# A graph layer on one core: the order of the first blocks, and a block's list of destinations spread by one full-width product

## The chip, the core and the metric

The kernel runs on one core of one Trainium2 chip. The core has five engines with queues of their own: PE (TensorE, matrix products), DVE (VectorE), ACT (ScalarE), POOL (GpSimd) and SP (SyncE, which here only issues transfers). Each engine works through its instructions in the order in which the program lists them, and waits on semaphores for the others. ACT, POOL and SP also issue DMA transfers. The metric is the device time of one execution in microseconds (us), as the median of several runs; one more execution was taken with the hardware profiler.

## What is computed

One layer of a graph network with a layer norm in front. There are 12,500 nodes with 64 features and 212,500 edges, sorted by their second end `dst` (the inputs are sorted so). Cut to what matters:

```python
h = relu(layernorm(x))                              # (12500, 64)
edge_in = concatenate([h[src], h[dst], weight])     # (212500, 129)
e = silu(edge_in @ eW1 + eb1)                       # (212500, 128)
e = silu(e @ eW2 + eb2)
agg = segment_sum(e, src, 12500)                    # sum over the edges of each first end
z = silu(concatenate([h, agg]) @ nW1 + nb1)
out = x + z @ nW2 + nb2
```

## The kernel before, in words

The first product is split by linearity. For each node the kernel projects `h` once with the upper half of `eW1` (table `ta`, for `src`) and once with the lower half (table `tb`, for `dst`), each as a rounded part and a remainder, so that a row has 2 x 128 numbers. Nodes are dealt to 100 buckets (`NB`), 125 to each.

**First half: edges to buckets.** The edges, in the order of `dst`, are cut into 208 blocks of 1024 (`BLK`); two blocks make a pair. Because `dst` is sorted, the 2048 edges of a pair need only a short stretch of rows of `tb`. `load` (L347) reads four windows of 60 rows of that stretch (`STEP` = 25 apart) into the tile `win`, two windows on partitions 0 to 59 and two on 64 to 123; next to them on each half stand three rows for the edge weight (two parts) and the bias. For each block `count` (L364) makes the list on DVE: which bucket each edge has (`oh`, `each`), how many came before it (`terms`, `rank`), and so the row of the buffer `q` to which it goes (`to`). `spread` (L337) puts the destinations of the block, as offsets into the windows (`rowsD`), on all partitions with two products, one for each half of 64 partitions, each with a column of the identity as its weights; `picked` (L373) compares them with the partition's own number (`same`) and adds the edge weights (`extras`). That gives `pick`, with one column for each edge. `send` (L440) multiplies `pick` with `win` on PE (`qp`), copies the result and the edge's place in its bucket to `qs` on ACT, and scatters the 128 rows of each tile to `q` with an indirect DMA on POOL (L476). `send_all` (L497) interleaves `send(s)` with `count(s + 1)` in three pieces for each block, and calls `load(s + 2)`.

**Second half: buckets to sums.** The buckets are read back from `q` in 14 levels (`LEVELS`), four buckets at a time, as soon as a level can no longer get rows (`fetch`, L523). A pipeline of steps (`turn`, L654) adds the `ta` row of the first end (`s_pt`), applies the two `silu` and the second product (`s_p2`, with the bias tile `b2f`), and sums by node with a one-hot product (`s_seg`). The last level continues into the node product (`nodes`, L274).

**The order.** PE, DVE, ACT and SP are scheduled by hand: instructions stand in the order in which the Python code makes them. The main loop (L886) walks over the steps and, at each `None` of `turn`, draws pieces of `send_all` so that each level's blocks are done when it starts. The projection of the nodes (`loaded`, `normed`, `products`, called the feed here) comes as generators through `turns`, and a fixed number of turns is drawn for each piece.

**The start.** The first blocks must not wait for all of `tb`. So 16 rows of x for each partition (`x0`, 2048 nodes) are loaded first, normalised (`norm`, L658) and projected by four calls of `first_rows` (L689) into a table of their own, `tb0`, which the windows of the first 30 blocks (`EARLY`) are read from. `sources` (L765) turns `src` into bucket and place (`bkt`, `locE`) for one half of each pair at a time; `destinations` (L742) makes the bases of the pairs' windows (`base_i`, read by SP at L355) and the offsets `rowsD`; `edge_weights` (L784) splits the weights into two parts, the second by a subtraction on POOL, and writes both to `ews`, from which `load_rows` (L328) reads each pair's `extras`. All of them have one pair on each partition (104 pairs, `NP`). `order` (L829) lists in which sequence turns of these generators stand, before the first block. `checks` (L792) makes sure that every destination lies in its window; if not, a slow general path runs at the end.

Of the kernel before, what the change touches and what calls it, by code (L numbers as in the profile page):

```python
# [28 lines left out]
F32 = mybir.dt.float32  # L29
# [48 lines left out]
def tile_gnn(ctx: ExitStack, tc: tile.TileContext, x, src, dst, ew, eW1, eb1, eW2, eb2, nW1, nb1, nW2, nb2, out):  # L78
# [48 lines left out]
    NE, EARLY = 16, 30  # L127
# [9 lines left out]
    dstR = lp.tile([NP, PAIR], I32, name="dstR")  # L137
    f, sf, t = (lp.tile([NP, PAIR], F32, name=n) for n in ("f", "sf", "t"))
    fv = f.rearrange("p (g e) -> p g e", e=HALF)
    lo = lp.tile([NP, 4], F32, name="lo")  # L140
    ewR, ewH = (lp.tile([NP, PAIR], F32, name=n) for n in ("ewR", "ewH"))
    nc.vector.memset(srcR[96:NP, LAST:], N)
    nc.vector.memset(ewR[96:NP, LAST:], 0.0)
    ones = const.tile([1, P], F32, name="ones")
# [3 lines left out]
    nc.sync.dma_start(x0, x[: NE * P, :].rearrange("(p j) d -> p j d", j=NE))  # L148
# [5 lines left out]
    for to, v, queue in ((srcR, src, nc.sync), (ewR, ew, nc.scalar), (dstR, dst, nc.sync)):  # L154
        for p0, p1 in ((0, 96), (96, NP - 1)):
            queue.dma_start(to[p0:p1, :], vec(v, p0 * PAIR, p1 - p0, PAIR))
        queue.dma_start(to[NP - 1 : NP, :LAST], vec(v, (NP - 1) * PAIR, 1, LAST))
    last = bass.AP(tensor=dst.tensor, offset=dst.offset + E - FEW, ap=[[PAD, 1], [0, PAD // FEW], [1, FEW]])
    nc.scalar.dma_start(dstR[NP - 1 : NP, LAST:].rearrange("p (r e) -> p r e", e=FEW), last)
# [25 lines left out]
    nc.vector.scalar_tensor_tensor(same, plus, -float(HB), part, op0=OP.mult, op1=OP.add)  # L185
    nc.vector.tensor_scalar(plus, same, float(WL + 2), None, op0=OP.is_equal)
# [20 lines left out]
    rowsD = const.tile([NP, 2, 2, HALF], BF16, name="rowsD")  # L207

    tb0 = dram.tile([P * NE, 2 * H], F32, name="tb0")
    ta_buckets, tb_buckets = (t.rearrange("(l b) f -> l b f", b=NB) for t in (ta, tb))  # L210
# [21 lines left out]
    base_i = const.tile([1, NP], I32, name="base_i")  # L232
    NW = 3
    wins = [const.tile([P, 2, 2, 2, H], F32, name=f"win{i}") for i in range(NW)]
    for win in wins:
        nc.vector.memset(win, 0.0)
# [15 lines left out]

    def later_weights():

        nc.gpsimd.dma_start(w2, eW2)
# [48 lines left out]
    with ExitStack() as work:  # L304
# [23 lines left out]
        def load_rows(s):  # L328

            if s < nblocks:  # L330
                p, g = s // 2, s % 2
                if g == 0:
# [4 lines left out]
        def spread(s):  # L337

            if s < nblocks:
                p, g = s // 2, s % 2  # L340
                bc = mm.tile([P, HALF], F32, name="bc", tag="mm")
                for a in range(2):
                    of = identb[:NP, p : p + 1].to_broadcast([NP, HB])
                    nc.tensor.matmul(bc[a * HB : (a + 1) * HB], of, rowsD[:, a, g], start=True, stop=True)  # L344
# [713 lines left out]
```

## Time and profile before

| | us |
|---|---|
| median of the runs (3) | 2402.55 |
| lowest, highest | 2399.72, 2406.02 |
| the profiled execution | 2402.95 |
| its span, first to last instruction | 2401.2 |

Busy time of the engines in the profiled execution: PE 2084.7 us (87% of the span), weight loads of PE 1909.0 (80%), DVE 1807.1 (75%), POOL 1655.6 (69%), ACT 1316.8 (55%). A busy PE is not a PE at its peak, because products are pipelined and the clock that it is granted changes (0.915 in the mean).

How to read the rows that follow. A row of the timeline has the start in us from the first instruction, the duration, engine, source line, operation, and what it writes and reads; in brackets stands how long its engine had been idle and what ended that. `SPq`, `ACTq` and `PEq` are the sequencers of these engines. A group has the count, busy time in total, the mean of one in ns, and the idle time ahead of it. A window has for each engine the busy time and the count, then the granted clock of PE, the busy share of the DMA engines, and GB/s. A row of waits has the total, the number and the longest.

### The profile page before, as it was taken

The page shows a single profiled execution, that of the slowest core. Times are in us where ns is not written, and L with a number is a line of the kernel's source. Part 1 is how long each engine was busy: PE and PEld are TensorE (multiplying, and loading weights), DVE is VectorE, ACT ScalarE, POOL GpSimd, SP SyncE. Part 2 cuts the span into 40 slices and gives each one's busy share as a digit, 9 for nine tenths or more (in the row PEclk, how much of TensorE's full clock was granted, in tenths as well). Part 3 has the DMA queues.
Part 4 walks back from the last instruction along what each step waited for, and adds up shares of the span by engine and source line. Part 5 has one row for each costly group of instructions (what it writes and reads, how often), then busy time and mean ns, then how long its engine had stood idle before and what let it go on. Part 6 is the DMA issues. An engine that isn't in the chain of part 4 may idle for free.

```text
span 2401.2 us, 47870 instructions
## 1 busy us (share of the span) xinstructions
PE 2084.7 (87%) x17025; PEld 1909.0 (80%) x17025; DVE 1807.1 (75%) x2852; ACT 1316.8 (55%) x2861; POOL 1655.6 (69%) x1723
## 2 busy tenths in 40 slices
PE   3777887666688889988999999999999999999997
PEld 2555676655588788888888999998999999999885
DVE  7989977766678787776877667899988888875221
ACT  3333444333355566656666767666666666666543
POOL 5667777777777777777777766777777777776110
PEclk9555698877889999999999999999999999999999
DMA  5565877666677666777777777988888888888663
GB/s 161 210 235 212 274 227 236 209 209 220 210 250 253 209 225 221 225 236 255 258 259 247 264 251 254 294 262 255 269 269 275 266 267 279 263 270 269 207 187 92
DMA packets 238859, 572.33 MB, mean 238 GB/s; under 512 B 46346, under 2 KB 98534, under 8 KB 238097
## 3 DMA queue, kind: packets, MB, share of 16 engines
q1 hardware_dynamic: 154598, 390.24, 51.8%
q0 software_dynamic: 54080, 124.64, 14.2%
q10 hardware_dynamic: 29936, 54.31, 6.9%
q8 instruction: 138, 2.26, 0.4%
q14 instruction: 107, 0.88, 0.1%
HBM read 356.62 MB, written 212.35 MB: 237 GB/s over the span
## 4 chain that ended last, share of the span: by engine, by line
PE 43%; DMA 19%; POOL 10%; DVE 7%; issue 5%; ACT 4%; SPq 1%; ACTq 0%; POOLq 0%; DVEq 0%
DMA q<-qs,to 16%; PE seg L636 10%; POOL q L476 10%; PE p L622 10%; PE pt L583 9%; PE pt L576 5%; PE qp L454 4%; PE lr L562 3%; DMA out_dram<-os 2%; PE bc L344 1%; ACT qs L466 1%; DVE one L605 1%; SPq L124 1%; ACT e L592 1%; DVE rank L414 1%
## 5 line engine op out<-in xcount | busy, mean ns | idle before, releaser
L476 POOL DMA_INDIRECT q<-qs,to x1661 | 1615.7, 973 | 565.5 <-issue 398.4
L583 PE MATMUL pt<-oneT,a 125*128 125x128 f32 (+1 forms) x2800 | 433.9, 293 | 143.1 <-ACT oneT L567 142.1
L592 ACT ACTIVATE e<-pt 128x512 f32<-128x512 f32 x450 | 268.8, 597 | 477.4 <-PE pt L583 471.9
L622 PE MATMUL p<-w,e 128*128 128x128 f32 x3600 | 513.4, 287 | 0.0
L636 PE MATMUL seg<-one,e 128*128 128x125 f32 x3600 | 508.9, 285 | 0.2 <-DVE aggT L647 0.2
L583 PEld LDWEIGHTS pt<-oneT,a 125*128 125x128 f32 x2800 | 365.8, 198 | 159.5 <-ACT oneT L567 157.8
L622 PEld LDWEIGHTS p<-w,e 128*128 128x128 f32 x3600 | 457.6, 198 | 22.4 <-issue 22.4
L636 PEld LDWEIGHTS seg<-one,e 128*128 128x128 f32 x3600 | 445.3, 195 | 28.7 <-issue 27.3
L466 ACT COPY qs<-qp 128x512 f32<-128x512 f32 x418 | 244.5, 586 | 392.3 <-DMA q<-qs,to 276.1
L647 DVE TENSOR_TENSOR aggT<-aggT,seg 128x500 f32<-128x500 f32 x325 | 218.5, 672 | 210.1 <-PE seg L636 208.0
L454 PE MATMUL qp<-win,pick 128*128 128x256 f32 x1664 | 329.1, 325 | 28.3 <-DVE pick L376 10.8
L605 DVE TENSOR_TENSOR one<-misc,qt 128x500 f32<-128x500 f32 x450 | 302.7, 673 | 60.0 <-PE seg L636 33.1
L395 DVE TENSOR_REDUCE each<-oh 128x100 bf16<-128x800 bf16 x208 | 321.1, 1544 | 7.2
L454 PEld LDWEIGHTS qp<-win,pick 128*128 128x128 f32 x1664 | 254.1, 213 | 48.2 <-issue 15.1
L576 PE MATMUL pt<-ident,qt 128*128 128x128 f32 x1800 | 276.5, 277 | 8.3 <-ACT qs L466 7.9
L626 ACT ACTIVATE e<-p 128x512 f32<-128x512 f32 x450 | 268.7, 597 | 25.6 <-PE p L622 25.2
L567 ACT CAST oneT<-lr 125x512 fp32r<-125x512 f32 x450 | 264.7, 588 | 12.8 <-PE lr L562 12.4
L616 ACT COPY p<-b2f 128x512 f32<-128x512 f32 x450 | 267.2, 594 | 0.0
L576 PEld LDWEIGHTS pt<-ident,qt 128*128 128x128 f32 x1800 | 209.6, 143 | 23.7 <-issue 12.2
L414 DVE TENSOR_REDUCE rank<-terms 128x8 f32<-128x864 f32 x208 | 219.0, 1053 | 7.2
L376 DVE SCALAR_TENSOR_TENSOR pick<-bc,same,extra 128x512 fp32r<-128x512 f32 x208 | 154.6, 743 | 82.4 <-PE bc L344 54.3
L412 DVE TENSOR_TENSOR terms<-oh,misc 128x800 f32<-128x800 bf16 x208 | 203.6, 979 | 6.2 <-PE misc L400 5.9
(142 smaller groups left out, 1662.8 us busy)
## 6 DMA issues: line engine op xcount, KB each, us to landing
a<-ta SPq DMA_DIRECT2D x350, 512.0 KB
qt<-q SPq DMA_DIRECT2D x250, 288.0 KB
qt<-q SPq DMA_DIRECT2D x100, 576.0 KB
q<-zeros ACTq DMA_DIRECT2D x25, 1080.0 KB
q<-qs,to POOLq DMA_INDIRECT x1661
win<-tb SPq DMA_DIRECT2D x208, 120.0 KB
tb<-got SPq DMA_DIRECT2D x29, 512.0 KB
q<-zeros ACTq DMA_DIRECT2D x20, 720.0 KB
```

Of the source, the lines that this page charges most:

```text
L395: nc.vector.tensor_reduce(each, oh.rearrange("p t b -> p b t"), AX.X, OP.add)
L454: nc.tensor.matmul(qp[:, t % 2, :k], halves(pick[:, t * P : (t + 1) * P]), halves(win[:, :k, v]), start=v == 0, stop=v == 1,)
L466: nc.scalar.copy(qs[:, ts, :k, :H], qp[:, ts, :k, :])
L476: ins = nc.gpsimd.indirect_dma_start(out=q[:], out_offset=bass.IndirectOffsetOnAxis(ap=to[:k, j : j + 1], axis=0), in_=qs[:k, t % 2, a, :] ...
L576: nc.tensor.matmul(pt[:, t, :], qt[:, j, :H], ident, is_transpose=True, start=t == 0, stop=False, skip_group_check=True)
L583: nc.tensor.matmul(pt[:, cols, :], halves(a[:L, b, i * H : (i + 1) * H]), halves(oneT[:, cols, :]), start=False, stop=i == 1, skip_group_c ...
L592: nc.scalar.activation(e1, pt, AF.Silu)
L605: nc.vector.tensor_tensor(one.rearrange("p (b j) l -> p b j l", j=n), spots[:, None, None, :].to_broadcast(wide), loc[:, tiles[0][1] : til ...
L616: nc.scalar.copy(p2, b2f)
L622: nc.tensor.matmul(p2[:, t, :], e1[:, t, :], w2, start=False, stop=t == G - 1, skip_group_check=True)
L626: nc.scalar.activation(e2, p2, AF.Silu)
L636: nc.tensor.matmul(item[2][:, b, :], e2[:, t, :], one[:, t, :], start=j < G, stop=j >= G * (n - 1))
```

## The change

Five things change together.

1. **The table of destinations.** `dstR`, `f` and `rowsD` no longer hold one pair on each of 104 partitions, but use all 128: partitions 0 to 63 hold, for 64 pairs, the parts of the lists that belong to the lower half of `win`, partitions 64 to 127 those for the upper half; pairs 64 to 103 are a second such table (`NT` = 2). The bases come from a small tile of each pair's first destination, `firstR`, loaded apart with rows of four bytes. `destinations` converts and subtracts one table at a time.
2. **The spread.** For each pair `load` now lets ACT write a table `sel` (128 x 128, one column of the identity for each half), and `spread` is one product over all rows and columns instead of two.
3. **The first rows.** `x0` is loaded in two parts, 512 nodes and 1536. The first call of `first_rows` writes its rows twice, to `tb0` and to `tb00`, from which the windows of the first two pairs are read. The other three calls move from the start into the feed.
4. **The order of the start.** `order` is shorter; `load(0)` and the beginning of `count(0)` come before the rest of `sources` and `later_weights`; the loads of the feed's first rows come after `count(0)`. The weights of pair 0 are read from the on-chip tiles instead of `ews`. In the first block two turns of the feed are drawn for each piece instead of four.
5. **`b2f` and `checks`.** The bias tile is loaded on POOL's queue with the other weights and multiplied before the first block is sent, instead of after the eighth. `checks` makes its reductions in eight turns, one for each quarter, instead of two.

```diff
-    for to, v, queue in ((srcR, src, nc.sync), (ewR, ew, nc.scalar), (dstR, dst, nc.sync)):
+    for to, v, queue in ((srcR, src, nc.sync), (ewR, ew, nc.scalar)):
...
+    for T in range(NT):
+        for a in range(2):
+            whole = min(HB, NP - T * HB) - (a == 1 and T == NT - 1)
+            for n0, n1 in ((0, HB // 2), (HB // 2, HB)):
+                n1 = min(n1, whole)
+                of = shown(T * HB + n0, n1 - n0, a * HALF, [[BLK, 2], [1, HALF]])
+                nc.sync.dma_start(dstR[a * HB + n0 : a * HB + n1, T], of)
+            n = min(HB, NP - T * HB)
+            nc.scalar.dma_start(firstR[a * HB : a * HB + n, T : T + 1], shown(T * HB, n, 0, [[1, 1]]))
...
+    row = const.tile([P, 2], F32, name="row")
+    nc.vector.tensor_copy(row[:, 0:1], same)
+    nc.vector.tensor_scalar(row[:, 1:2], plus, float(STEP), None, op0=OP.mult)
...
+                if s == 0:
+                    for i, v in enumerate((ewH, ewR)):
+                        for a in range(2):
+                            at = a * HB + WL + i
+                            of = v[0:1].rearrange("p (g a e) -> p g a e", g=2, a=2)[:, :, a]
+                            nc.sync.dma_start(extras[0][at : at + 1], of)
...
-                for a in range(2):
-                    of = identb[:NP, p : p + 1].to_broadcast([NP, HB])
-                    nc.tensor.matmul(bc[a * HB : (a + 1) * HB], of, rowsD[:, a, g], start=True, stop=True)
+                nc.tensor.matmul(bc, sels[p % NW], rowsD[:, p // HB, g], start=True, stop=True)
...
+                if s < 2 * FIRST_PAIRS:
+                    table, end = tb00, G * P
...
+                    of = identb[:, p % HB :: HB][:, :, None].to_broadcast([P, 2, HB])
+                    nc.scalar.copy(sels[p % NW].rearrange("p (a m) -> p a m", a=2), of)
...
+            for to in ([tb00.rearrange("(p j) f -> p j f", j=G)] if g == 0 else []) + [rows]:
+                nc.sync.dma_start(to, got.rearrange("p g k h -> p g (k h)"))
...
+            yield
+            base = lp.tile([P, NT], F32, name="base")
+            nc.vector.tensor_copy(base, firstR)
+            nc.vector.tensor_tensor(base, base, lim, op=OP.min)
+            lot = mm.tile([1, NT, P], F32, name="lot", tag="mm")
+            for T in range(NT):
+                nc.tensor.transpose(lot[:, T, :], base[:, T : T + 1], ident)
...
+            for T in range(NT):
+                if T:
+                    nc.scalar.copy(f[:, T], dstR[:, T])
...
+                for j in range(2 * NT):
+                    nc.vector.tensor_reduce(ends[:, i, j : j + 1], fv[:, j : j + 1, :], AX.X, op)
+                    yield
...
-            order = [rows_, weights, rows_, made[0], src0, made[0], src0, made[1], made[0], made[0], src0, made[1], lists_]
-            order += [made[2], made[1], made[1], src0, made[2], lists_, made[3], made[2], made[2], src0, made[3], lists_]
-            order += [made[3], made[3], src0, lists_, src1]
+            order = [rows_, rows_, made[0], src0, made[0], src0, weights, lists_, made[0], made[0], src0, src0, lists_]
+            order += [lists_, src0, src0]
             for part_ in order:
                 next(part_)
+            load(0)
+            load_rows(0)
+            for part_ in (count0, lists_, src1, count0):
+                next(part_)
             for win in wins[1:]:
                 last_rows_of(win)
             later_weights()
...
+            for _ in range(2):
+                p2 = p2p.tile([P, G, H], F32, name="p2")
+                nc.tensor.matmul(p2, ones, b2f[0:1], start=True, stop=True)
+                nc.scalar.copy(b2f, p2)
+            for _ in count0:
+                pass
+            for _ in range(2):
+                list(todo.pop(0))
             load(1)
             rest = turns(todo, 3)
-            feed = itertools.chain(itertools.islice(rest, 48), checks(), rest)
-            for _ in send_all(0, 2 * FIRST):
-                for _ in range(4):
+            feed = itertools.chain(turns(made[1:], 2), itertools.islice(rest, 40), checks(), rest)
+            for i, _ in enumerate(send_all(0, 2 * FIRST)):
+                for _ in range(2 if i < PIECES else 4):
                     next(feed, None)
```

96 lines of the change are left out of this document (50 added, 46 removed).

## The prediction

> **What bounds the kernel now.** I read the page first, then the windows of one line, then the windows of all engines, then the timeline of the start. The largest group of the page is the scatter of edge rows on POOL:
>
> ```profile
> span 2401.2 us, 47870 instructions
> L476 POOL DMA_INDIRECT q<-qs,to x1661 | 1615.7, 973 | 565.5 <-issue 398.4
> ```
>
> 1661 scatters at 0.973 us, and before most of them 0.3 us of issue. The windows of that line alone say where this pace is kept (stretch, its length, busy us, count, clock, DMA share, GB/s):
>
> ```profile
> 43.50:163.20 119.70, 73.20 (x73) 0.56 0.54 191
> 163.20:1285.00 1121.80, 853.84 (x879) 0.87 0.72 234
> 1285.00:1417.00 132.00, 100.56 (x104) 0.99 0.77 254
> 1417.00:1600.00 183.00, 124.05 (x129) 1.00 0.83 272
> 1600.00:2211.00 611.00, 464.08 (x479) 1.00 0.83 268
> 2211.00:2401.00 190.00, 0.00 (x0) 0.97 0.55 166
> ```
>
> 879 scatters in 1121.8 us and 479 in 611.0 us are both 1.276 us each: there the queue never starves. It loses time in three places only: before the first scatter; from 43.5 to 163.2, where 73 scatters need 93.1 us and 26.6 us are lost; and from 1417 to 1600, where 129 need 164.6 and 18.4 are lost. After the last one a tail of 190 us remains. So the end is start + 1661 x 1.276 + losses + tail, and the change, whose moved work lies in the first 160 us, can be read in these terms. Who sets the pace in each stretch (PE, PEld, DVE, ACT, POOL busy):
>
> ```profile
> 43.50:163.20 119.70, 80.49 (x370) 57.71 (x370) 100.98 (x173) 43.62 (x119) 73.20 (x73) 0.56 0.54 191
> 250.00:1285.00 1035.00, 846.34 (x6729) 774.78 (x6727) 787.76 (x1200) 541.06 (x1173) 787.46 (x812) 0.90 0.72 234
> 1285.00:1600.00 315.00, 307.94 (x2785) 296.14 (x2786) 238.20 (x369) 212.17 (x446) 224.60 (x232) 0.99 0.80 264
> 1600.00:2211.00 611.00, 597.83 (x5411) 571.86 (x5411) 520.80 (x801) 385.52 (x830) 464.08 (x479) 1.00 0.83 268
> ```
>
> In the first row DVE is busy 101.0 of 119.7 us and PE 80.5: DVE, which makes each block's list and also the feed (normalising and projecting the nodes), starves POOL. From 250 to 1285 PE has 18% idle while POOL is full: PE follows the scatters. From 1285 PE is 98% busy and its own bound; its program interleaves pieces and steps in a fixed order, so if POOL and PE both come to that point earlier, everything behind shifts with them.
>
> **The start.** The timeline (start, duration, engine and line; in brackets what it waited for):
>
> ```profile
> 2.56 0.91 DVE L236 MEMSET win<- 128x1024 f32 x1 [0.18 <-issue]
> 9.68 1.21 DVE L663 TENSOR_REDUCE mean<-x 128x16 f32<-128x1024 f32 x1
> 16.74 1.90 ACT L786 CAST ewH<-ewR 104x2048 fp32r<-104x2048 f32 x1 [1.59 <-DMA ewR<-in_edge_weight_dram]
> 18.79 1.23 DVE L774 SCALAR_TENSOR_TENSOR sf<-t,sf 104x1024 f32<-104x1024 f32 x1
> 21.83 4.54 POOL L787 TENSOR_TENSOR ewR<-ewR,ewH 104x2048 f32<-104x2048 f32 x1
> 30.94 0.33 SPq L696 DMA_DIRECT2D tb<-got  x1
> 31.96 0.98 DVE L387 TENSOR_TENSOR oh<-misc,bkt 128x800 bf16<-128x800 f32 x1
> 37.08 1.01 SPq L360 DMA_DIRECT2D win<-tb  x2
> 38.20 1.14 SPq L335 DMA_DIRECT2D extra<-ews  x4
> 40.42 0.75 DVE L376 SCALAR_TENSOR_TENSOR pick<-bc,same,extra 128x512 fp32r<-128x512 f32 x1 [3.30 <-DMA extra<-ews]
> 43.52 1.90 POOL L476 DMA_INDIRECT q<-qs,to  x1 [14.59 <-ACT qs L469]
> ```
>
> DVE runs from the first mean at 9.68 to the end of the list at 37.1, then `pick` waits 3.30 us for the edge weights, and 3.1 us after it stands the first scatter.
>
> Added ahead of the mean: two memsets of 1024 elements on 32 partitions (each as the 0.91 us row, with its 0.16 gap 2.1 us) and six small ones for `row` and `lim`, some 0.15 each: +3.0 us, mean at 12.7, `sf` done at 23.0 instead of 20.0. Removed between `sf` and `oh`: three of the four `first_rows` with the waits between them. Before, that stretch is 20.0 to 32.0. Now `oh` waits for ACT, whose order is square, `sf`, root, `hr`, `got`, `ewH`, half of `f`, two `bkt`. By the rate of the `ewH` row (1.90 us for 2048 columns), `ewH` runs 22.9 to 24.8, `f` 1.0, the two `bkt` 0.5 each: `oh` at 27.0, 4.9 us earlier. The second half of `rowsD` (1.2 us) now stands after `each`: the list ends at 33.6, 3.5 earlier. Moved ahead of the first `qp` on PE are the two products for `b2f`; at 2.04 us each (row further down) with two ACT copies they end near 34.7, so they hide behind the list to within a microsecond.
>
> The new wait is data for `pick`. The weights of pair 0 come from the on-chip rows, but `ewR` needs the 4.54 us subtraction on POOL, now 24.8 to 29.4, because `ewH` is later. On SP the extras stand behind two writes of `got` (`tb00`, `tb0`), the register load and both `win` loads. Before, the last `got` write went out at 30.94 and the `win` load that waits for it at 37.08, 6.1 us for 0.5 MB, with the two 0.85 MB `ews` writes of L789 alongside. Now `got` goes out near 24, so `tb00` lands between 27 and 30; but the `ews` writes start at 29.4 and meet the `win` loads and extras (2.2 us before, from 38.20 to 40.42). Lower bound: no contention, the list decides, `pick` at 33.6. Upper: the loads wait until the `ews` writes are through, 6 to 7 us after issue, `pick` at 38. I take 36.4, nearer the upper, since the only row of the kind shows a slow landing. First scatter 39.5 instead of 43.5: **-4.0 us, bounds -6.8 to -2.4**.
> By the Trainium skill's "DMA: Bandwidth & Descriptors", section on queues, rings and completion order, each DMA engine goes round its queues packet by packet, so SP's loads would not wait for POOL's writes to be through; by that, -6.8 and a total 2.8 us lower. The 6.1 us row leans the other way.
> The queues it is moved past: SP issues ten destination loads instead of three, at about the 0.33 us of the `got` write, done before 12; ACT's queue gets four loads of 4-byte rows, for which no row exists, but they have until 24 (if late by 3 us, the list is late by 3). The `xs` loads go out after the extras, near 31 instead of 14, and are first used in block 2 or 3, near 55. POOL issues the `b2f` load and three more `win` row loads ahead of the subtraction, about 2 us, and is free near 24, as `ewH` ends.
>
> **The first blocks.** The stalls of POOL between 43.5 and 163.2, and what lies behind them:
>
> ```profile
> 54.73 1.21 POOL L476 DMA_INDIRECT q<-qs,to  x1 [5.46 <-ACT qs L469]
> 64.26 0.97 POOL L476 DMA_INDIRECT q<-qs,to  x1 [3.87 <-ACT qs L469]
> 97.77 2.29 DVE L796 TENSOR_REDUCE ends<-f 104x4 f32<-104x2048 f32 x1
> 113.57 0.97 POOL L476 DMA_INDIRECT q<-qs,to  x1 [6.36 <-ACT qs L469]
> 145.47 2.04 PE L858 MATMUL p<-b2f,ones 1*128 1x512 f32 x2 [4.83 <-DMA b2f<-in_L_gnn_eb_dram]
> 152.45 0.97 POOL L476 DMA_INDIRECT q<-qs,to  x1 [7.77 <-ACT qs L469]
> ```
>
> The costs of DVE in that window (group, busy us, mean ns, idle before):
>
> ```profile
> L395 DVE TENSOR_REDUCE each<-oh 128x100 bf16<-128x800 bf16 x10 | 15.2, 1519 | 0.3
> L414 DVE TENSOR_REDUCE rank<-terms 128x8 f32<-128x864 f32 x9 | 9.5, 1053 | 0.3
> L227 DVE TENSOR_TENSOR got<-ab,got 128x256 f32<-128x256 f32 x25 | 9.6, 417 | 3.6 <-ACT got L224 3.5
> L376 DVE SCALAR_TENSOR_TENSOR pick<-bc,same,extra 128x512 fp32r<-128x512 f32 x9 | 6.7, 742 | 7.1 <-PE bc L344 7.1
> ```
>
> The 7.77 us stall at 152.45 is the `b2f` chain: PE waited 4.83 for its DMA, multiplied twice and let `pick` wait 7.1. Loaded and multiplied before the first scatter, it is gone. The 6.36 us stall at 113.57 lies behind `checks`, which took DVE for two reductions of 2.29 us in one piece. The new one makes eight of about 0.6 us in eleven turns, four to a piece: same work, shorter holds. The two stalls of the first blocks (5.46, 3.87) came from ACT waiting on the normalisation of `xs`; now ACT has `bkt`, `locE`, `hr`, `got` there, and the second half of block 0 still needs the whole `src1` chain, so 4.4 us remain of the first and little of the second.
>
> What keeps the rest from vanishing is DVE. One list costs 5.95 us (the eight operations from `oh` to `pick`; the longest rows stand above), nine make 53.6, so 47.4 of the 101.0 are feed: checks 5.2, `src1` 3.3, and 38.9 for 93 turns, 0.42 each. After: turns in the first eight blocks are 90 (two a piece in the first block), of which 11 are checks and 12 the three moved `first_rows` (3 x 2 x 0.417 = 2.5), so 67 x 0.42 = 28.0; feed 39.0, DVE 92.6 against POOL's 91.8 for 72 scatters. With some 9 us of waits left (11.6 now without `pick`'s 7.1), DVE needs 101.6: **9.5 us lost instead of 26.6, -17.1**. Bounds: 2 lost if the waits overlap (-24.6), 19 lost if only `b2f`'s stall goes (-7.6). The feed turns not done here run over blocks 9 to 23 instead of 9 to 20, nine turns to a block: 3.8 + 5.95 us, under 10.2. If that cover failed, 0.4 us a turn would be lost.
>
> **The spread.** In the PE-bound stretch, on PE alone:
>
> ```profile
> 1450.90 0.41 PE L344 MATMUL bc<-rowsD,identb 104*64 104x512 bf16 x2
> 1451.24 1.16 PE L622 MATMUL p<-w,e 128*128 128x128 f32 x8
> 1452.23 0.40 PE L562 MATMUL lr<-identb,one 128*125 128x128 bf16 x4
> 1452.46 1.11 PE L636 MATMUL seg<-one,e 128*128 128x125 f32 x8
> ```
>
> The two half-width products take 0.34 us until the next instruction starts; four `lr` products, also 512 rows of bf16 in sum, take 0.23. One full-width product should be like the latter: 0.11 us per block, 29 blocks between 1285 and 1600 (104 + 129 scatters over 8), up to 3.2 us off the 18.4 lost there; nothing after 1600, where POOL is full. The Trainium skill's "TensorE: Matmul & The Clock Gate", part on packing small matmuls, has column tiles run side by side for the price of one; the pair starts as one entry here and agrees, and by that rule the merged product saves nothing. I take half, -1.6.
> The table costs ACT one copy of 128x128 per pair. Nearest rows:
>
> ```profile
> L469 ACT CAST qs<-locE 128x64 f32<-128x64 bf16 x414 | 105.2, 254 | 0.0
> L466 ACT COPY qs<-qp 128x512 f32<-128x512 f32 x414 | 243.5, 588 | 392.3 <-DMA q<-qs,to 276.1 <-PE qp L454 82.3 <-PE lr L562 10.6
> ```
>
> and what PE waits for on ACT between 1285 and 1600 (total, times, longest):
>
> ```profile
> PE pt L583 <- ACT oneT L567: 3.0, 1, 3.0
> ```
>
> 0.25 to 0.59 us, I take 0.3, 104 times. It is queued two blocks before its use, ahead of a `qs` eviction. Until 1285 POOL's backlog of eight `qs` tiles covers it; from 1285 ACT is two thirds busy and PE waited for it once. Cost 0; uncovered, 45 pairs x 0.3 = 13.5 us.
>
> **Sum.** -4.0 - 17.1 - 1.6 = -22.7 us. The profiled execution took 2402.95 us (span 2401.2), 0.4 above the median of 2402.55 (2399.72 to 2406.02): 2402.95 - 22.7 = 2380.3, on the median's scale **2380 us**.
>
> **Rivals.**
> *DVE gives only the named wait back* (0.17). Its work stays the pace, and the other stalls return in other places: -7.6 - 2.4 = -10, 2393 us. For it: 84% busy. Against: the moved turns take 8.4 us off DVE there.
> *The gain stops at PE* (0.06). Were PE the bound through the whole middle, an earlier scatter would only wait longer: 2402 us. Against: 18% idle from 250 to 1285.
> *ACT's copies lengthen the PE-bound half, slower* (0.06). If a copy costs like the 128x512 row and each ACT microsecond there holds back a `qs` eviction and with it PE: 45 x 0.59 = 26.5 us against 21.1 gained, 2408 us. It decides from 0.47 us exposed per pair up. Against: ACT's idle third.
> *More* (0.09). Start -6.8, first blocks -24.6, spread -3.2: -35, 2368 us.
>
> **How the numbers follow.** The forecast gets 0.62, with 2371 to 2389 as its own range. Of the -10 case most lies below the bound of faster. The range 2366 to 2396 takes in the bounds of start and first blocks and the -10 case, and leaves out the two last-named losses and part of the 2368. A change under 0.3% (7 us) can't be told from none. Faster by more than that: 0.62 + 0.09 + most of 0.17 = 0.86; within 0.3%: 0.09; slower: 0.05.
>
> **What would show it.** First scatter between 37 and 41, `pick` just before it waiting for the extras; from there to the 73rd scatter about 101 us with no stall over 5 except one after the fourth scatter; no `b2f` product after the first scatter; `checks` rows near 0.6 us; then 1.276 us each to about 1395, 15 to 18 us lost within 200 us, last scatter near 2187, the tail 190. The `bc` row should be one product of about 0.23 to 0.34 us, the table copy about 0.3. I am wrong if the first scatter is not earlier, if new stalls over 5 us appear in the first ten blocks or near 230, where the feed now meets the first steps, or if more than 22 us are lost from 1285 to 1600.

## The result, and the profile after

The median fell from 2403.45 us (four runs, 2399.72 to 2406.02) to 2385.22 us (four runs, 2383.31 to 2388.04). The ratio of the runs is 0.9928, with a 95% interval of 0.9913 to 0.9943 (the two medians alone give 0.9924). The medians differ by 18.2 us, where 22.7 were forecast. The profiled execution of after took 2388.04 us, the longest of its four, so the two traces differ by 14.9 us only, and the terms below add up to that number.

The page of after, its span and the scatters:

```profile
span 2386.3 us, 47571 instructions
L513 POOL DMA_INDIRECT q<-qs,to x1661 | 1617.5, 974 | 545.7 <-issue 396.7
```

The windows of the scatter line (stretch, length, busy us, count, clock, DMA share, GB/s), cut at the places that answer to those of before:

```profile
41.70:146.70 105.00, 73.29 (x73) 0.68 0.55 194
146.70:1268.00 1121.30, 853.88 (x878) 0.87 0.72 237
1390.00:1585.00 195.00, 133.96 (x139) 1.00 0.82 271
1585.00:2195.00 610.00, 463.62 (x478) 1.00 0.83 269
```

The first of these windows over all engines (PE, PEld, DVE, ACT, POOL):

```profile
41.70:146.70 105.00, 69.28 (x330) 52.19 (x331) 94.45 (x164) 39.54 (x110) 73.29 (x73) 0.68 0.55 194
```

Read them in the terms of the forecast. The first scatter stands at 41.70 (43.52 before): -1.8. From there the 73rd comes 105.0 us later (119.7): -14.7. From the 73rd to 1390 the lead shrinks from 16.5 to 15.3 us, +1.2: 878 scatters take 1121.3 us, 1.277 each, where 1.276 was the pace before. From 1390 to 1585, 139 scatters need 177.4 us at 1.276 and take 195: 17.6 lost instead of 18.4, and the last scatter goes out at 2193.1 (2209.2), 16.1 ahead: -0.8. The tail is 193.2 us instead of 192.0: +1.2. The sum is -14.9.

**The start.** The timeline of after:

```profile
25.34 4.52 POOL L835 TENSOR_TENSOR ewR<-ewR,ewH 104x2048 f32<-104x2048 f32 x1 [2.86 <-ACT ewH L834]
26.23 4.71 DVE L808 TENSOR_TENSOR rowsD<-f,lo 128x1024 bf16<-128x1024 f32 x1 [1.18 <-ACT f L793]
29.81 0.56 POOL L837 DMA_DIRECT2D ews<-ewH  x1
31.05 3.67 SPq L366 DMA_DIRECT2D extra<-ewR  x2
33.29 1.21 DVE L808 TENSOR_TENSOR rowsD<-f,lo 128x1024 bf16<-128x1024 f32 x1
36.98 0.17 DVE L453 TENSOR_SCALAR to<-rank 128x8 int32<-128x8 f32 x1
38.60 0.75 DVE L413 SCALAR_TENSOR_TENSOR pick<-bc,same,extra 128x512 fp32r<-128x512 f32 x1 [1.45 <-DMA extra<-ewR]
41.70 1.90 POOL L513 DMA_INDIRECT q<-qs,to  x1 [10.79 <-ACT qs L506]
```

and the same subtraction on DVE in the timeline of before:

```profile
27.80 1.22 DVE L757 TENSOR_TENSOR rowsD<-f,lo 104x1024 bf16<-104x1024 f32 x1
```

Two things are late. The first subtraction of the offsets took 4.71 us instead of 1.22 (the second, at 33.29, took 1.21 again). It runs from 26.23 to 30.94, and POOL's subtraction of the weights from 25.34 to 29.86: DVE's ends 1.08 us after POOL's, about its own duration. In before POOL's stood at 21.83 to 26.37, and DVE's first at 27.80; the new order put them side by side. So the list ends at 37.15, as in before (37.12), and not at 33.6. And `pick` then still waits, to 38.60, for the extras, so that it is these that set the first scatter: SP needed 3.67 us to issue two small loads at 31.05, while the two `ews` writes, the first of which POOL had issued at 29.81, were on their way.

**The first blocks.** The four stalls of POOL of over 1.5 us that are left, in its timeline (the scatter behind each):

```profile
50.56 0.97 POOL L513 DMA_INDIRECT q<-qs,to  x1 [3.09 <-ACT hr L723]
67.71 0.97 POOL L513 DMA_INDIRECT q<-qs,to  x1 [1.80 <-ACT qs L506]
91.85 0.97 POOL L513 DMA_INDIRECT q<-qs,to  x1 [2.98 <-ACT qs L506]
125.69 0.97 POOL L513 DMA_INDIRECT q<-qs,to  x1 [2.74 <-ACT got L248]
```

None is over 3.1 us. Those of 6.36 and 7.77 us behind `checks` and `b2f` are gone. DVE is busy 94.5 us of the 105.0.

**The spread.** PE around a block's product, before and after, at the same place of the program (timelines; x4 and x8 are runs of equal instructions):

```profile
1450.33 0.64 PE L454 MATMUL qp<-win,pick 128*128 128x256 f32 x4
```

```profile
1449.27 0.63 PE L491 MATMUL qp<-win,pick 128*128 128x256 f32 x4
1449.74 0.39 PE L377 MATMUL bc<-rowsD,sel 128*128 128x512 bf16 x1
1449.97 1.05 PE L659 MATMUL p<-w,e 128*128 128x128 f32 x8
```

Before, 0.57 us go from the first `qp` to the pair and 0.34 from the pair to what follows (1450.90, 1451.24), 0.91 in all; after, 0.47 and 0.23, 0.70. The one product saves 0.21 us, of which 0.10 lie ahead of it. Over the 58 places of this kind that each trace has in the last stretch (behind 1600 and behind 1585), the medians of the whole are 0.98 and 0.79.

### The profile page after: what moved, and what is told of

Its sections match the earlier page's. It is cut to its first block, busy times and chain, and to the rows that moved or that the text cites. A ratio compares the mean times of both kernels' runs of the same rounds, so it can differ in the third digit from the quotient of the medians.

```text
span 2386.3 us, 47571 instructions
## 1 busy us (share of the span) xinstructions
PE 2039.2 (85%) x16818; PEld 1913.8 (80%) x16818; DVE 1811.5 (76%) x2865; ACT 1336.1 (56%) x2966; POOL 1657.6 (69%) x1724
## 4 chain that ended last, share of the span: by engine, by line
PE 40%; DMA 19%; DVE 13%; POOL 9%; issue 6%; ACT 5%; SPq 2%; ACTq 0%; DVEq 0%; POOLq 0%
DMA q<-qs,to 15%; PE p L659 10%; POOL q L513 9%; PE seg L673 9%; PE pt L620 8%; PE qp L491 4%; PE pt L613 4%; DMA out_dram<-os 3%; PE lr L599 2%; DVE rank L451 2%; DVE each L432 2%; DVE one L642 1%; DVE oh L424 1%; DVE terms L449 1%; ACT qs L503 1%
## 5 line engine op out<-in xcount | busy, mean ns | idle before, releaser
L659 PEld LDWEIGHTS p<-w,e 128*128 128x128 f32 x3600 | 465.2, 200 | 15.7 <-issue 14.9
L673 PEld LDWEIGHTS seg<-one,e 128*128 128x128 f32 x3600 | 449.9, 195 | 19.2 <-issue 17.6
L424 DVE TENSOR_TENSOR oh<-misc,bkt 128x800 bf16<-128x800 f32 (+1 forms) x209 | 203.7, 975 | 2.4 <-ACT bkt L829 2.4
```

What stands on the lines that cost most here:

```text
L659: nc.tensor.matmul(p2[:, t, :], e1[:, t, :], w2, start=False, stop=t == G - 1, skip_group_check=True)
L673: nc.tensor.matmul(item[2][:, b, :], e2[:, t, :], one[:, t, :], start=j < G, stop=j >= G * (n - 1))
```

## The experiments

Nine kernels were run, in twelve runs, and all of them met chips on which the kernel before takes 1.39 to 1.42 times as long (3340 to 3422 us). From about 55 us on, engines stand there for up to 16.3 us at a time for something that the profile does not name. A row of the waits of one of them, 300 to 1270 us (total, times, longest):

```profile
ACT e L627 <- remote: 138.2, 16, 14.8
```

In after nothing of the kind stands in that stretch. The start is not touched by it: where the edit leaves after's order of the start, the first scatter is at 41.4 to 42.1 (41.70). So these runs are read for the first 60 us, for the duration of single instructions, and for ratios; single times scatter by 15 us either way and settle little.

**One input for the offsets.** To see whether the second input of DVE's subtraction is what makes it wait for POOL:

```diff
-                nc.vector.tensor_tensor(
-                    rowsD[:, T], f[:, T], lo[:, T, :, None].to_broadcast([P, 2, HALF]), op=OP.subtract
-                )
+                for g in range(2):
+                    nc.vector.tensor_scalar(rowsD[:, T, g], f[:, T, g], lo[:, T, g : g + 1], None, op0=OP.subtract)
```

> The offsets rowsD are made by four DVE subtractions with the base as a scalar for each partition (one input from SBUF) instead of two with two inputs from SBUF; nothing else changes. Theory (port): in the changed kernel the first rowsD took 4.71 us instead of 1.22 because POOL's subtraction of the edge weights ran from 25.34 to 29.86 and both read SBUF through something they share; with one input the first two run at once, about 0.6 us each, while POOL subtracts, and the list ends near 33.5 instead of 37.1. The first scatter then still moves by less than 1 us from 41.7, because pick waits for the extras of ewR (38.6) and qp for the b2f products (38.4). Rival (data): rowsD waited for something else, and takes as long here. Rival (list): the list alone set the start, and the first scatter comes 3 to 4 us earlier, at 38.

The timeline, and the durations of the four halves (min, median, max in ns):

```profile
25.63 4.52 POOL L834 TENSOR_TENSOR ewR<-ewR,ewH 104x2048 f32<-104x2048 f32 x1 [2.86 <-ACT ewH L833]
26.52 4.36 DVE L809 TENSOR_SCALAR rowsD<-f,lo 128x512 bf16<-128x512 f32 x2 [1.18 <-ACT f L793]
36.56 0.17 DVE L453 TENSOR_SCALAR to<-rank 128x8 int32<-128x8 f32 x1
38.62 0.75 DVE L413 SCALAR_TENSOR_TENSOR pick<-bc,same,extra 128x512 fp32r<-128x512 f32 x1 [1.88 <-DMA extra<-ewR]
```

```profile
L809 DVE TENSOR_SCALAR rowsD<-f,lo x4: 476/502/3910, 26.5 to 33.6; 128x512 bf16<-128x512 f32 x4
```

A miss: with one tensor input the first half still took 3.91 us, to 0.28 us after POOL's end, and only the other three took 0.5. So it is not the second input alone that makes it wait. It settles something else, though: the list ended 0.42 us earlier (36.73 instead of 37.15), and `pick` did not, 38.62. In this start the extras decide.

**The whole start without its waits.** ACT makes the offsets, the `ews` writes go out on SP behind the extras, and `b2f` is filled by a transfer alone (two products remain behind block 8, whose result is not read; the check of the windows reads the offsets):

```diff
-                if T:
-                    nc.scalar.copy(f[:, T], dstR[:, T])
-                nc.vector.tensor_tensor(
-                    rowsD[:, T], f[:, T], lo[:, T, :, None].to_broadcast([P, 2, HALF]), op=OP.subtract
-                )
+                for g in range(2):
+                    nc.scalar.activation(rowsD[:, T, g], dstR[:, T, g], AF.Identity, bias=lo[:, T, g : g + 1])
...
-                nc.gpsimd.dma_start(ews[i], v.rearrange("p (g a e) -> p g a e", g=2, a=2))
...
             load_rows(0)
+            for i, v in enumerate((ewH, ewR)):
+                nc.sync.dma_start(ews[i], v.rearrange("p (g a e) -> p g a e", g=2, a=2))
```

> The changed kernel with three waits of its start taken away at once: ACT makes rowsD straight from dstR with the negative base as its bias (no copy to f, nothing on DVE, checks reduce rowsD instead), the writes of ews go out on SP behind the extras of pair 0 instead of on POOL ahead of them, and b2f is loaded onto all partitions by DMA instead of being spread by two products (two short products only open its PSUM tiles). Theory: the list ends near 32.5 and pick waits for the extras until 33 to 35, so the first scatter stands at 36 to 38 instead of 41.7, and as DVE is the pace up to block 9 and has 2.4 us less to do, block 9 starts 4 to 7 us earlier than 146.6; this lasts to the end. Rival (landing): extras and win loads land no earlier without the ews writes beside them, pick stays at 38 and the first scatter at 41.

```profile
25.10 4.53 POOL L829 TENSOR_TENSOR ewR<-ewR,ewH 104x2048 f32<-104x2048 f32 x1 [2.36 <-ACT ewH L828]
25.85 1.33 ACT L804 ACTIVATE rowsD<-dstR,lo 128x512 bf16<-128x512 int32 x2
25.87 0.99 DVE L422 TENSOR_TENSOR oh<-misc,bkt 128x800 bf16<-128x800 f32 x1 [1.06 <-ACT bkt L823]
28.36 1.42 DVE L442 TENSOR_TENSOR alike<-bkt 128x64 bf16<-128x64 bf16 x1
30.28 1.17 SPq L364 DMA_DIRECT2D extra<-ewR  x2
32.05 0.17 DVE L451 TENSOR_SCALAR to<-rank 128x8 int32<-128x8 f32 x1
32.59 0.75 DVE L411 SCALAR_TENSOR_TENSOR pick<-bc,same,extra 128x512 fp32r<-128x512 f32 x1 [0.36 <-DMA extra<-ewR]
35.70 1.89 POOL L511 DMA_INDIRECT q<-qs,to  x1 [6.07 <-ACT qs L504]
```

The list ends at 32.22 and the first scatter stands at 35.70, 6.0 us ahead of after. Beside POOL's subtraction ACT's halves take 0.7 each. But `alike`, which compares two on-chip tables and took 0.28 in after, takes 1.42 and ends at 29.78, 0.15 us after POOL: another instruction with two inputs from on-chip tables, the same wait. `oh`, which has one input from there and one from the memory that PE writes its products to, took 0.99 beside the same subtraction (0.98 in after), so not every DVE instruction waits. No run took the subtraction off POOL; that DVE waits for it is read from the ends of these rows, 0.15 to 1.09 us behind POOL's, and from the same work at its usual length where POOL does not subtract.

**One wait of the start alone.** After, with only the two `ews` writes moved to SP behind the extras:

> The kernel of after with one thing moved: the two writes of the weights to memory go out on SP behind the extras and not on POOL ahead of them. Theory 'the writes delay the extras': the extras land within 2 us of their issue, pick follows the list at 37.2 without a wait, first scatter 40.2 to 40.4 (41.70 in after); the offsets on DVE still take 4.7 us beside the subtraction on POOL, so it does not come down to the 35.7 of the version without either. Rival 'the extras are late for another reason' (the loads of the feed, the windows, the subtraction): pick still waits for them, first scatter 41 to 42.

```profile
26.34 4.72 DVE L808 TENSOR_TENSOR rowsD<-f,lo 128x1024 bf16<-128x1024 f32 x1 [1.18 <-ACT f L793]
31.17 1.17 SPq L366 DMA_DIRECT2D extra<-ewR  x2
33.27 7.43 SPq L741 DMA_DIRECT2D xs<-in_x_dram  x4
37.09 0.17 DVE L453 TENSOR_SCALAR to<-rank 128x8 int32<-128x8 f32 x1
36.45 2.07 PE L894 MATMUL p<-b2f,ones 1*128 1x512 f32 x2 [0.68 <-ACT b2f L895]
37.28 0.75 DVE L413 SCALAR_TENSOR_TENSOR pick<-bc,same,extra 128x512 fp32r<-128x512 f32 x1
38.45 1.22 PE L491 MATMUL qp<-win,pick 128*128 128x256 f32 x4
40.74 1.54 POOL L513 DMA_INDIRECT q<-qs,to  x1 [10.77 <-ACT qs L506]
```

Issuing the two loads takes 1.17 us instead of 3.67, and `pick` follows the list without a wait. The first scatter stands at 40.74 instead of 41.70. So the two writes, as they stood in after, made that wait. The run changes both their place and their queue, and does not tell which of the two counts. The wait also moves on: the four `xs` loads, now behind the writes, take 7.43 us to issue instead of 3.24, and the next loads of extras go out at 43.37 instead of 38.17. Of the 1.3 us that `pick` gains, 0.4 are given back: `pick` is done at 38.03, but `qp` starts at 38.45, about when PE is through with `b2f`'s second product (36.45 + 2.07), which is the next to be late. The subtraction still took 4.72, and `pick` now follows the list. So the waits of the start lie side by side: taking one away shows the next, and the 35.70 was seen only with all of them gone.

**Does the start's gain last?** The version without the waits was timed twice against the kernel before, in five rounds each:

> The whole kernel of after with the three waits of its start taken away (offsets made by ACT, the writes of the weights on SP behind the extras, b2f filled by a transfer); now timed against the kernel before. Theory 'the queue of scatters is the sum': what the start gains is kept, since the middle runs at the queue's pace and the stretch held by PE shifts with it: first scatter near 35.7 (41.70 in after), 73rd near 141 (146.7), last scatter near 2187.5 (2193.1), time 2379 to 2381 us, 0.990 of before. Rival 'the start is hidden': DVE, whose work for the first nine blocks is unchanged, or PE takes the lead back: lead over after at the 73rd scatter under 2 us, time 2384 to 2387. Rival 'more': the checks read the offsets as half-wide numbers and ACT takes 2.4 us off DVE, so another 2 to 4 us are gained in the first blocks: 2375 to 2378.

> The version without the three waits of the start once more, to see whether its lead of 5.6 to 6.0 us at the first scatter is there at the end. If the times of the kernel before are again near 2403 us: theory 'the start is kept': first scatter 35.5 to 36.1, 73rd scatter 140 to 142 (146.7 in after), last scatter 2186 to 2189 (2193.1), time 2378 to 2381, 0.990 of before (after stands at 0.9928). Rival 'hidden by DVE': the 73rd scatter at 145 or later and a time of 2384 to 2387. Rival 'hidden by PE': 73rd scatter near 141, but the stretch 1390 to 1585 loses 23 to 25 us instead of 18.8, time 2383 to 2386. If the times of the kernel before are near 3344 again, only the first 60 us and the ratio count: 5.6 of 3344 is a ratio of 0.992 to 0.995.

First scatters at 36.07 and 35.75. The first time it took 3327.07 us against 3344.32 (ratio of the runs 0.9933, 0.9908 to 0.9957), the second time, on another chip, 3324.99 against 3340.49 (0.9951, 0.9924 to 0.9978). Both intervals lie below 1. Whether it beats after was not measured: after was not timed on these chips, and its own ratio of 0.9928 comes from undisturbed ones.

The 73rd scatter, expected near 141, stands at 157.1, 154.2 and 155.2 in the three runs of this kernel. In two kernels with after's feed on the chip of the second of these, one with the `ews` writes moved and one with two products in the spread (below), it stands at 154.7 and 157.6. The lead over the former is 4.7 us at the first scatter, 3.6 at the 65th, 0.5 at the 73rd, 5.1 at the 81st and 3.5 at the last one (3136.35 against 3139.85), and single runs there scatter by more than that. The rival that DVE hides the start is not refuted, and it stays open what part of the 6 us arrives.

**Two products again.** After, with the spread undone to two products of 64 columns, from the new table:

```diff
-                nc.tensor.matmul(bc, sels[p % NW], rowsD[:, p // HB, g], start=True, stop=True)
+                for a in range(2):
+                    half = slice(a * HB, (a + 1) * HB)
+                    nc.tensor.matmul(bc[half], sels[p % NW][:, half], rowsD[:, p // HB, g], start=True, stop=True)
```

> The changed kernel with the spread alone undone: the same tables, but two products of 64 columns each instead of one of 128. Theory: PE saves about 0.2 us per block by the full-width product (from the last qp product to the instruction behind the spread 0.348 us instead of 0.546), but POOL's queue caps what comes of it. So the scatters run as in the changed kernel up to 1285 (within 1 us at block 150), the loss from 1268 to 1600 is 0 to 2 us more than the 18.8 there, and the time is 0 to 3 us longer. Rival: PE is the bound from 1285 to the last scatter; then 110 blocks at 0.2 us, and the last scatter comes 15 to 20 us later. Second rival: the width is worth nothing, because the saving comes from elsewhere; then 0.348 us stays.

> The kernel of after with two products of 64 columns in the spread instead of one of 128, all else as in after. Theory 'capped': the pair costs 0.2 us more on PE for each of 208 blocks (41 us), but only where PE sets the pace does it reach the end: the stretch 1390 to 1585 loses 20 to 23 us instead of 18.8, last scatter 1 to 4 us later than in after, time 2386 to 2389 us. Rival 'nothing': PE's idle time takes it all, 2385. Rival 'all of the PE-bound part': from 1270 on every block costs 0.2 us more up to the end of the steps, so besides the 29 blocks before 1585 the tail is longer too: 29 x 0.2 = 6 us and more, 2391 to 2396.

The same stretch of PE in the second of these, and in the version with the `ews` writes moved, which ran on the same chip with the one product:

```profile
2018.87 0.71 PE L493 MATMUL qp<-win,pick 128*128 128x256 f32 x4
2019.51 0.41 PE L379 MATMUL bc<-rowsD,sel 128*64 128x512 bf16 x2
2019.85 0.66 PE L615 MATMUL pt<-ident,qt 128*128 128x128 f32 x4
```

```profile
2015.29 0.72 PE L491 MATMUL qp<-win,pick 128*128 128x256 f32 x4
2015.84 0.39 PE L377 MATMUL bc<-rowsD,sel 128*128 128x512 bf16 x1
2016.07 0.60 PE L613 MATMUL pt<-ident,qt 128*128 128x128 f32 x4
```

From the first `qp` to the instruction behind, 0.98 us with two products and 0.78 with one: 0.20 us for each block, from the products alone. The time was 3335.85 us against 3344.32 (ratio of the runs 0.9982, 0.9960 to 1.0004), and the first of the two runs took 3411.61 against 3422.36. What the 0.20 us are worth at the end can't be told from these: the version without the waits, at 3327.07 on the same chip, differs in the start as well.

**The first blocks.** Three kernels put back one or both of the edits to `b2f` and `checks` in after: the products of `b2f` behind block 8, the reductions in two pieces, and both.

```diff
-            for _ in range(2):
-                p2 = p2p.tile([P, G, H], F32, name="p2")
-                nc.tensor.matmul(p2, ones, b2f[0:1], start=True, stop=True)
-                nc.scalar.copy(b2f, p2)
...
+        for _ in range(2):
+            p2 = p2p.tile([P, G, H], F32, name="p2")
+            nc.tensor.matmul(p2, ones, b2f[0:1], start=True, stop=True)
+            nc.scalar.copy(b2f, p2)
...
-                for j in range(2 * NT):
-                    nc.vector.tensor_reduce(ends[:, i, j : j + 1], fv[:, j : j + 1, :], AX.X, op)
-                    yield
+                nc.vector.tensor_reduce(ends[:, i, :], fv, AX.X, op)
```

> The changed kernel with the two b2f products put back behind the eighth block; the load stays early, so no DMA is waited for. Theory: the chain of two products of 2.07 us and two ACT copies holds PE and ACT there for about 5 us, and as DVE has no slack at that place, a stall of 4 to 5.5 us of POOL appears before the ninth block; block 12 starts 4 to 5 us later than in the changed kernel, and it stays so to the end. The first scatter comes 0 to 1 us earlier than 41.7. Rival: only the wait for the DMA (4.83 us before) made the stall; then less than 1.5 us is lost.

> The changed kernel with the reductions of checks in one piece each again (two turns instead of eight; the same elements). Theory (hold): two reductions of about 2.3 us one behind the other hold DVE, and with it pick, so a stall of 3 to 6 us of POOL appears around block 5 or 6 and block 9 starts 3 to 5 us later. Rival (throughput): DVE is full in the first nine blocks, its work there is the same or, because six turns of the feed come earlier, 2 to 3 us more; then the stalls only move, and block 9 starts 1 to 3 us later at most. Rival (nothing): within 1 us.

> The kernel of after with b2f's products back behind block 8 and checks back in two reductions of a whole table's length. First scatter as in after (41.7), since the wait there is for the extras. Theory 'the prediction's accounting': their two stalls come back at their old places (after the fourth and eighth block, 5 to 7 us each), the 73rd scatter is 10 to 13 us later than in after (157 to 160 instead of 146.7), and the order of the first rows alone is worth some 5 us. Rival 'DVE only': b2f's and checks' stalls take up waits that DVE has anyway, and the 73rd scatter is less than 6 us later (under 153); then the moved first rows and the fewer turns of block 0 were the main part.

First scatters at 41.76, 41.93 and 41.85: `b2f`'s products at the start cost the first scatter nothing as long as `pick` waits for the extras. The timeline of POOL in the third, at the scatters behind the whole `checks` and behind `b2f` (the 45th and the 65th), and below it the 65th in the kernel of one input, which has both edits as after:

```profile
113.58 0.97 POOL L513 DMA_INDIRECT q<-qs,to  x1 [3.27 <-ACT qs L506]
152.15 0.97 POOL L513 DMA_INDIRECT q<-qs,to  x1 [10.19 <-ACT qs L506]
```

```profile
147.70 0.97 POOL L513 DMA_INDIRECT q<-qs,to  x1 [3.06 <-ACT qs L506]
```

A stall behind `b2f` comes back: 10.19 us of idle, and the two products with their copies stand right ahead of it, from 145.14 to 150.58; it was 7.77 in before and is 0.30 in after. Its size can't be given to `b2f` alone. With `b2f` alone put back the 65th scatter waits 6.52 us, with `checks` alone 5.92, and in two kernels of the same chip as these, with both edits as after, 3.06 and 2.57. Behind the whole `checks` stand 3.27 and, alone, 3.28 us; the kernel of one input has a stall of 2.72 four scatters on, so little can be seen there.

The 73rd scatter is at 160.9 with either one put back, against 158.8 and 159.8 in the two kernels of that chip: 1 to 2 us later, less than was expected of each. With both it is at 162.9, against 154.7 and 157.6 on its chip: 5 to 8 us later, short of the 10 to 13 of the first expectation. The chips' own stalls lie in this stretch (the 57th scatter waits 6.35 us in the kernel of one input and 2.74 in after), so the split stays open.

**Two more.** The kernel before with only the `b2f` chain moved to its start, and after with three turns of the feed for each piece instead of four:

> The kernel before with only the b2f chain moved: its load early on POOL's queue, its two products before the first block is sent. Theory: the stall of 7.8 us before the ninth block goes, the first scatter moves by less than 1 us, and from block 9 on every scatter is 6.5 to 8 us earlier than before, to the end. Rival (DVE is full anyway): the stall's removal is taken back by DVE within the next blocks, and less than 4 us is left at block 20.

> The changed kernel with three turns of the feed for each piece instead of four in blocks 1 to 7. Theory (throughput): DVE's work is the pace of the first nine blocks (93.8 of 105.0 us busy from the first scatter to block 9); a turn costs 0.42 us of DVE, three fewer per block take 1.26 us off each of seven blocks, so of the 13 us that POOL loses before block 9 some 6 to 9 go, block 9 starts 6 to 9 us earlier than 146.6, and the turns left over cost nothing later, because nine turns and a list (9.7 us) stay under POOL's 10.2. The time falls by as much. Rival (waits): the stalls come from single waits of ACT and DVE for each other; then block 9 moves by less than 2 us. Rival (pushed on): the gain is given back between blocks 9 and 30, when the feed meets the first steps, and the last scatter does not move.

3405.98 and 3403.86 us against 3414.24, one run each. In the first, the first scatter stands at 42.90, so the two products can lie before it in the old order too, and the 65th waits 3.10 us (7.77 in before); its 73rd scatter at 170.5 can't be compared with 163.2 of an undisturbed chip.

In the second, up to the 73rd scatter, DVE is busy 85.8 us instead of 94.5. Four runs with four turns can be set beside it (one input, `ews` moved, two products twice). The 17th scatter stands at 69.1, among their 66.9 to 69.3, but the 73rd at 152.5 against their 154.7 to 159.8. So less work of DVE did bring the first blocks forward, by 2 to 7 us, where 6 to 9 were expected. It did not last: the 161st stands at 299.3 against their 292.9 to 295.9. These are single runs on several chips; on its own chip there is only the version without the waits, which is 4.6 us behind it at the 73rd, for all its lead at the start, and 6.7 ahead at the 161st.

## Why the prediction was right, and where it was off

The sign, the size class and the place were right: 2385.22 lies 5.2 us above the 2380 and inside the likeliest case's own range, the first 73 scatters give 14.7 of the 14.9 us while the other terms cancel, and the middle runs at its old pace. By its own steps:

- **Start, -4.0 forecast, -1.8 measured, outside the bounds of -6.8 to -2.4.** The step that failed is the landing of the extras: `pick` was to start at 36.4, with 38 as the upper bound, and started at 38.60. These 2.2 us are the whole difference. The wait itself was foreseen, and the upper case was the right one: the loads waited with the `ews` writes ahead of them, and with these behind them they landed 1.1 us after their issue (32.59 against 30.28 + 1.17) instead of 3.9 (38.60 against 31.05 + 3.67). By the round of packets that the prediction took from the Trainium skill's "DMA: Bandwidth & Descriptors", section on queues, rings and completion order, there was to be no such wait and `pick` would have followed the list; the 38.60 against 37.15 decides otherwise here.
- **List at 33.6, measured 37.15.** A second step failed and was hidden behind the first: the row of `rowsD`, carried over at 1.2 us from a place where POOL did not subtract to one where it does. The working had both on the page, "4.54 us subtraction on POOL, now 24.8 to 29.4" and `oh` at 27.0, and costed neither against the other. `oh` began at 30.86, 3.9 later, of which 3.5 are the subtraction on DVE. The Trainium skill's "SBUF — State Buffer", section "Who interferes with whom", has this: DVE and GpSimd share one pair of ports, locked for a whole instruction by the one that starts first, against a DVE instruction that has two inputs in SBUF (the memory of the on-chip tables) or runs in a mode that takes both ports, for which it names `tensor_scalar`. The 4.71, the 3.91 of the one-input form and the 1.42 of `alike` agree with it; that the one-input form ran in such a mode is not shown by any run.
- **First blocks, -17.1 forecast, -14.7 measured.** The mechanism held: no stall over 5 us, the `b2f` stall gone, and DVE's work near the pace, as the run with fewer turns bears out. The size was off: 105.0 us to the 73rd scatter where the sum over DVE gave 101.6, with DVE busy 94.5 instead of 92.6 and idle 10.5 instead of 9. The 101.6 is 18.1 under the 119.7 of before, not 17.1, so the miss by the prediction's own figures is 3.4 us. How the gain splits over the five edits was not settled.
- **Spread, 0.11 us a block and half of it taken.** Mis-sized on PE: 0.20 are saved, 0.10 of them ahead of the product where the forecast did not look. The term at the end, -1.6, came out at -0.8. The traces suggest why more did not arrive. The steps' `e` on ACT, the 196th and the 271st, in the timelines of before and of after:

```profile
1310.95 0.60 ACT L592 ACTIVATE e<-pt 128x512 f32<-128x512 f32 x1 [1.22 <-PE pt L583]
1583.42 0.60 ACT L592 ACTIVATE e<-pt 128x512 f32<-128x512 f32 x1 [1.64 <-PE pt L583]
```

```profile
1299.06 0.60 ACT L629 ACTIVATE e<-pt 128x512 f32<-128x512 f32 x1 [0.83 <-PE pt L620]
1565.77 0.60 ACT L629 ACTIVATE e<-pt 128x512 f32<-128x512 f32 x1 [1.20 <-PE pt L620]
```

The steps are 11.9 us ahead on entering the PE-bound stretch and 17.6 on leaving it, 5.8 us gained. 22 blocks lie between, which at 0.20 us give 4.4 of it, so PE seems to have kept what the product saves. But POOL was 15.3 ahead on entering, so the first 3.4 only brought the steps level, and what passed 16.1 was not used, for behind 1585 the scatters keep their own pace. This is read from the two traces; no run tested it. The column rule of the Trainium skill's "TensorE: Matmul & The Clock Gate", by which the prediction had one product save nothing over the pair, does not hold here, by the 0.98 and 0.78 us.
- **ACT's table copy at nothing.** Right: 0.3 us, 104 times, and in after no wait of over 0.3 us is put down to it.
- **Tail at 190, unchanged.** 1.2 us longer; no run bears on it.

## What to carry to other kernels

When an edit moves instructions, lay the new order beside the other engines' rows and price each one where it will stand: the same DVE subtraction cost 1.2 us with GpSimd idle and 4.7 beside a subtraction on GpSimd. Here small loads that were needed next were late behind two large writes of another queue; look for such a pair before you price a start. And a lead at one place need not arrive at the end, so look for it further on: in one run fewer turns of the feed brought the 73rd scatter forward, and the lead was gone by the 161st.

## What the runs showed that was not expected

- DVE's subtraction beside a subtraction on GpSimd: 4.71 us instead of 1.22, and 3.91 instead of 0.5 for half of it with one tensor input; ACT's same work 0.7 a half beside it, and DVE's `oh` 0.99 (0.98 without).
- Two small loads on SP's queue took 3.67 us to issue and 3.9 more to land behind two 0.85 MB writes of POOL's queue; with the writes behind them and on SP, 1.17 and 1.1. In before a write of SP's went out in 0.33 us at 30.94, 4 us behind the same two, so what makes the issuing slow is not shown.
- A pair of 64-column products costs 0.20 us more here than one of 128 columns of the same length: 0.09 of that before the first of the pair starts (0.64 us from the first `qp` to it, against 0.55).
- All of the experiments' chips ran the kernel before 1.39 to 1.42 times as long, with waits of all engines for something outside the profile. Its cause was not found.
